# A twelve-layer decoder on one core: both ends of the state-space layer interleaved, and the norms, scores and last group of the last three layers moved

## The chip, the cores and the metric

The kernel runs on one core of a Trainium2 chip. The metric is the device time of one execution in microseconds; the median of three runs is used. The core has five instruction streams that run beside each other: TensorE (PE, matrix products and transposes, results in PSUM), VectorE (DVE), ScalarE (ACT), GpSimd (POOL) and SyncE (SP, which here only starts transfers). Each works through its own queue in order, and a semaphore makes an instruction wait for another engine or a transfer.

## The reference

A residual stream x of 32 sequences x 128 tokens x 128 channels (fp32) goes through twelve sublayers, each of them added to x after a norm without weights:

```python
def _layernorm(x, axis=-1, eps=1e-05):
    m = jnp.mean(x, axis=axis, keepdims=True)
    v = jnp.var(x, axis=axis, keepdims=True)
    return (x - m) / jnp.sqrt(v + eps)

x = x + _L0_attn_ref(_layernorm(x), ...)    # state-space layer (layer0 in the kernel)
x = x + _L0_xattn_ref(_layernorm(x), ctx, ...)  # 8-head attention over x and ctx (layer1)
...
x = x + _L3_attn_ref(_layernorm(x), ...)    # sparsemax attention on 32 patterns (layer9)
x = x + _L3_xattn_ref(_layernorm(x), ctx, ctx, dropout_mask, Wout, bout, 32)  # layer10
x = x + _L3_ffn_ref(_layernorm(x), weight_q, weight_scale, bias)              # layer11
```

The state-space layer has a projection, a causal convolution over four tokens, a gate, a decay dt per head, a scan over the tokens, a gated norm with weights and an output projection. The sparsemax attention needs 32 scores per head and token in sorted order:

```python
z_sorted = -jnp.sort(-z, axis=-1)
cum = jnp.cumsum(z_sorted, axis=-1)
tau = (cum_sel - 1.0) / k_sup          # from the largest k that is still in the support
A = jnp.maximum(z - tau, 0.0)
```

Layer10 is a softmax attention with a dropout mask: `softmax(x ctx^T / 32) * mask`, times ctx, times Wout. Layer11 quantizes each token to int8 by its largest absolute value, multiplies with int8 weights and scales back:

```python
x_scale = jnp.maximum(amax, EPS) / 127.0
x_q = jnp.clip(jnp.round(x2d / x_scale), -128, 127).astype(jnp.int8)
acc = x_q @ weight_q.T
out = acc * x_scale * weight_scale + bias
```

## The kernel before

**Tiling.** The 32 sequences are G = 8 groups of J = 4; `xg[i]` holds the residual of group i on 128 partitions (tokens) x 4 x 128, in place through the whole kernel. A "block" is one sequence of one group. Short-lived tiles come from small rings: `gmid` (10 buffers of 128x512), `bmid` (5), `bbig` (4 of 128x2048), `gbig` (3), `val`, `xn` and `xnT` (2), and in PSUM `ps`, `two` and `acc` (2 each). A tile that finds no free buffer waits until the last reader of the oldest one is done.

**Order.** The engines' queues are written out from the Python program. `Ordered` (L194 is the call in it, which is why nearly every row of the profile has that line) can tie an engine's instructions to the order of the program: `follow(T, A, V)` does so for TensorE, ACT and DVE in layer0 and in layer1. Outside of that a scheduler lays the order by its own estimates, so in the last layers the order of emission is only a hint. POOL and SP are never tied by `follow`.

**Start.** SP loads the constants `cs` (L278), then the eight groups of x (L284), three of the weight units (L304) and, since nothing holds it back, the int8 weights wq (L1691), although `layer9` writes that load. ACT's queue loads `first`, `wide`, `rows` and `small` (`ws`). DVE turns wq to bf16 once (L1692).

**layer0** runs round by round, one block per round: `first` (scores of the block and its POOL products, L805 to L812), `second`, `exponentials`, `weighted` and `third` are of consecutive blocks, and beside them the generators `conv` (four per group), `gate`, `entry` (the norm of a group), `decays` (dt) and `joined` (gated norm and output projection of a finished group) go forward by a step at a time through `go`. The loop begins at n = -9 with the steps of the first groups and ends with two rounds of `joined` for the last group. The power -1/2 of a norm is on POOL (L738, L891).

**layer1** then loads ctx (L323), normalizes (`prepare`, `normed` on POOL, L397), projects (`project_in`), makes scores, exponentials and the product with the reciprocal sum (L1020 on POOL), and enters its rounds: transposes of block n, scores of block n+1, values, `weighted`, `project_out`.

**layer9 to layer11** are one loop over i = 0 to 10 with 15 steps n each. In turn i, group i is sorted (`sort`, a merge network on DVE whose unchanged ends ACT copies), group i-1 gets its thresholds (`threshold`, TensorE, ACT, DVE and a POOL subtraction at L1753) and its `values`, group i-2 goes through layer10 and group i-3 through layer11. The norm of these three layers is `norm_act`: statistics on DVE, the power on POOL (L364), the shift on DVE, and the scaling on ACT, all emitted in one go. The scores of group i+1 are emitted at n = 10. The second half of the experts of layer8 lies in a list, `beside`, whose 49 entries are spread over the first 54 steps:

```python
slots = G // 2 * len(steps) - 6
```

In layer10 and layer11 POOL has the product with the mask (L1838), the scaling by the reciprocal sum (L1844), clipping and rounding (L1881, L1882) and the last two additions (L1896, L1897), for each group. The output of a group leaves from SP (L1898) behind its last addition.

Of the kernel before, what the change touches and what calls it, by code (L numbers as in the profile page):

```python
# [204 lines left out]
def program(ctx, tc, cols, x, ctxt, mask, drop, dfirst, dsmall, dwide, drows, dunits, dexperts, dconst, drel, dwq, out):  # L205
# [72 lines left out]
    SY.dma_start(out=cs, in_=dconst)  # L278
# [3 lines left out]
    for i in range(G):  # L282
# [3 lines left out]
        if i == 0:  # L286
            w0 = units.tile([128, cfirst.n], F32, tag="unit", name="w0")
            A.dma_start(out=w0, in_=dfirst)
            ww = const.tile([128, cwide.n], F32, name="ww")
            A.dma_start(out=ww, in_=dwide.to_broadcast([128, cwide.n]))  # L290
            wr = const.tile([1, crows.n], F32, name="wr")
            A.dma_start(out=wr, in_=drows)
# [27 lines left out]

    def load_ctx(i):
# [30 lines left out]
    def norm_act(src, o, by=None, by2=None):  # L352
# [6 lines left out]
        if by is not None:  # L359
            V.tensor_tensor(rs, mv[:, :, 1], by2, ALU.mult)  # L360
            V.tensor_scalar(rs, rs, EPS, None, ALU.add)
        else:
            V.tensor_scalar(rs, mv[:, :, 1], EPS, None, ALU.add)
        P.tensor_tensor(rs, rs, K["nhalf"], ALU.pow)  # L364
        if by is not None:
            V.tensor_tensor(rs, rs, by, ALU.mult)
        V.scalar_tensor_tensor(sh, mv[:, :, 0], -1.0, rs, ALU.mult, ALU.mult)
        for j in range(J):
            A.activation(o[:, j, :], src[:, j, :], AF.Identity, bias=sh[:, j : j + 1], scale=rs[:, j : j + 1])

    def layernorm_act(i):
        xn = mid.tile([128, J, D], F32, tag="xn", name="xn", bufs=2)
        xnT = mid.tile([128, 512], F32, tag="xnT", name="xnT", bufs=2)
        norm_act(xg[i], xn)
        transposed(xn, xnT, A.copy)
        return xnT
# [291 lines left out]
    def layer0():  # L668
# [190 lines left out]
        def joined(g):  # L859

            ys, sq = [], []
            for b in range(2):
                y = bmid((128, J, 128))
# [8 lines left out]
            for y in ys:  # L872
                q = bmid((128, J, 128))
# [10 lines left out]
            ln = bmid((128, J, 128))  # L884
            A.copy(ln, op)
            yield
# [21 lines left out]
        for n in range(-9, G * J + 2):  # L908
# [46 lines left out]
            go(conv, g, c)  # L955
        follow()

    def layer1(then):  # L960
# [12 lines left out]
        def project_in(n):  # L973
            i, j = n // J, n % J
            at = slice(j * 128, (j + 1) * 128)
            if n % 2 == 0:
                keys[n // 2] = gbig((128, 2, 4, 256))
# [81 lines left out]
        follow(T, A, V)  # L1059
        prepare(0, 0)  # L1060
        prepare(0, 1)
        project_in(0)
        for c2 in range(2):
            for step in scores(0, c2):
                step()
        prepare(1, 0)
        project_in(1)
        project_values(0)
        for n in range(last + 1):
# [10 lines left out]
            if n < last:  # L1080
# [12 lines left out]
                weighted(n)  # L1093
                if j == 0 and 0 < i and i + 1 < G:
# [3 lines left out]
        follow()  # L1098
# [590 lines left out]
    def layer9():  # L1689
        wq8 = const.tile([128, 32], I32, name="wq8")  # L1690
        SY.dma_start(out=wq8, in_=dwq)  # L1691
        V.tensor_copy(wq, wq8.bitcast(I8))  # L1692
# [16 lines left out]
        def scores(i):  # L1709
            xnT = layernorm_act(i)  # L1710
# [6 lines left out]
            ordered[i] = flat(z)  # L1717

# [36 lines left out]
        def values(i):  # L1755
            z = zs.pop(i)
# [22 lines left out]
            for j in range(J):  # L1779
                A.copy(yT[:, j], t[:, :, j])  # L1780
            project(i, yT.rearrange("p j h l -> p (j h l)"), W["a3_Wo"], WW["L3_attn_bo"])


        scores(0)
        queue = list(beside)
        slots = G // 2 * len(steps) - 6
        for i in range(G + 3):
            tails = {}
            if 0 <= i - 2 < G:
                tails |= dict(zip((1, 4, 7, 11), layer10(i - 2)))  # L1790
            if 0 <= i - 3 < G:
                tails |= dict(zip((2, 5, 8, 12), layer11(i - 3)))
            for n in range(len(steps)):
# [6 lines left out]
                if 0 <= i - 1 < G and n < 4:  # L1800
                    threshold(i - 1, n)
                if 0 <= i - 1 < G and n == 6:
                    values(i - 1)
                if i + 1 < G and n == 10:
                    scores(i + 1)
                if n in tails:
                    tails[n]()
# [9 lines left out]
    def layer10(i):  # L1817

        st = {}

# [130 lines left out]
```

## Time and profile before

| | us |
|---|---|
| runs (median of 3; lowest, highest) | 3045.65 (3045.08, 3048.45) |
| the profiled execution | 3068.78 |
| its span, first to last instruction | 3066.8 |

| engine | busy, us | share of the span |
|---|---|---|
| PE (matmul) | 2563.0 | 84% |
| PEld (weight load) | 1638.7 | 53% |
| DVE | 2086.1 | 68% |
| ACT | 1529.3 | 50% |
| POOL | 1007.4 | 33% |

The mean granted TensorE clock is 0.91. The chain of work that ended last is 49% PE, 31% DVE, 8% ACT and 6% POOL of the span. Landmarks: layer0's fill is over at about 65 us, its last block at about 443, layer1's rounds begin at 487, the first sort step stands at 2536.5, the later turns of the sort begin at 2573.4, 2641.8, 2715.1, 2778.8, 2831.9, 2888.3 and 2945.9, the last sort step ends at about 2991, and the last output is started at about 3063.

How to read it: in the slices each digit is the busy share of a fortieth of the span (77 us) in tenths; PEclk is the granted clock of TensorE in tenths. A row of the timeline begins with its start and its length, then engine, line, operation, output<-input by the program's names and shapes, and in brackets how long the engine was idle before it and what ended that. A row of waits has what waited, on what, the sum in us, how often, and the longest. A group's row has the count, the busy sum and the mean in ns of one.

### The profile page before, as it was taken

The page shows a single profiled execution, that of the slowest core. Times are in us where ns is not written, and L with a number is a line of the kernel's source. Part 1 is how long each engine was busy: PE and PEld are TensorE (multiplying, and loading weights), DVE is VectorE, ACT ScalarE, POOL GpSimd, SP SyncE. Part 2 cuts the span into 40 slices and gives each one's busy share as a digit, 9 for nine tenths or more (in the row PEclk, how much of TensorE's full clock was granted, in tenths as well). Part 3 has the DMA queues.
Part 4 walks back from the last instruction along what each step waited for, and adds up shares of the span by engine and source line. Part 5 has one row for each costly group of instructions (what it writes and reads, how often), then busy time and mean ns, then how long its engine had stood idle before and what let it go on. Part 6 is the DMA issues. An engine that isn't in the chain of part 4 may idle for free.

```text
span 3066.8 us, 55735 instructions
## 1 busy us (share of the span) xinstructions
PE 2563.0 (84%) x22535; PEld 1638.7 (53%) x22554; DVE 2086.1 (68%) x4254; ACT 1529.3 (50%) x3540; POOL 1007.4 (33%) x1042
## 2 busy tenths in 40 slices
PE   4887878999989999999998999988886869885564
PEld 2555556777744445556664444445553657543333
DVE  4776756888878856667776555468894329777883
ACT  3554544444422246666664444467771225555563
POOL 3333332322310113235441000223433445424544
PEclk7877878999999999999998999979997989998777
DMA  3000000000000000000000000000003243100000
GB/s 109 2 2 2 2 23 4 8 5 5 1 21 1 1 32 2 5 9 9 12 2 15 1 1 1 1 1 2 1 6 124 84 147 114 55 18 14 21 11 21
DMA packets 50147, 68.36 MB, mean 22 GB/s; under 512 B 3681, under 2 KB 41570, under 8 KB 49762
## 3 DMA queue, kind: packets, MB, share of 16 engines
q1 hardware_dynamic: 42608, 33.84, 3.6%
q0 software_dynamic: 6848, 27.81, 2.7%
q8 instruction: 178, 2.92, 0.4%
q10 hardware_dynamic: 434, 3.14, 0.3%
q14 instruction: 79, 0.65, 0.1%
HBM read 51.11 MB, written 13.68 MB: 21 GB/s over the span
## 4 chain that ended last, share of the span: by engine, by line
PE 49%; DVE 31%; ACT 8%; POOL 6%; issue 3%; DMA 1%; another core or an unknown queue 1%; SPq 0%; POOLq 0%; DVEq 0%; ACTq 0%
PE ps L194 22%; PE two L194 15%; PE acc L194 13%; DVE bbig L194 13%; DVE s L194 9%; DVE bmid L194 4%; DVE gmid L194 3%; ACT bbig L194 3%; POOL xn L397 3%; ACT bmid L194 2%; ACT gmid L194 1%; DVE x L194 1%; POOL s L395 1%; ACT gbig L194 1%; POOL s L364 1%
## 5 line engine op out<-in xcount | busy, mean ns | idle before, releaser
L194 PE MATMUL ps<-cs,bbig 128*128 128x128 f32 x2208 | 326.6, 287 | 82.0 <-ACT bbig L194 34.4
L194 PEld LDWEIGHTS ps<-cs,bbig 128*128 128x128 f32 x2208 | 251.8, 145 | 187.2 <-ACT bbig L194 81.0
L194 ACT COPY bbig<-ps 128x512 f32<-128x512 f32 x416 | 228.2, 590 | 247.2 <-PE ps L194 246.9
L194 DVE TENSOR_REDUCE s<-two 128x8 f32<-128x1024 f32 (+1 forms) x192 | 234.2, 1220 | 123.7 <-PE two L194 122.6
L194 DVE TENSOR_TENSOR bbig<-bbig 128x256 f32<-128x256 f32 (+4 forms) x394 | 274.0, 749 | 1.3 <-ACT bbig L194 0.3
L194 PE MATMUL two<-xnT,u 128*128 128x512 f32 x512 | 260.0, 608 | 11.8 <-ACT bmid L194 6.3
L194 PE MATMUL acc<-bmid,u 128*128 128x512 f32 x448 | 238.2, 619 | 32.8 <-DVE bmid L194 31.4
L194 PE MATMUL two<-gbig,gmid 32*128 32x512 f32 (+1 forms) x1280 | 223.1, 570 | 3.1 <-ACT bbig L194 2.4
L194 DVE TENSOR_TENSOR bmid<-bmid,ps 128x512 f32<-128x512 f32 x192 | 130.1, 684 | 108.3 <-ACT bmid L194 89.2
L194 ACT ACTIVATE bbig<-two,s 128x256 f32<-128x256 f32 (+1 forms) x512 | 189.7, 419 | 24.5 <-DVE s L194 21.2
L477 POOL TENSOR_SCALAR gbig<-bmid,cs 128x512 f32<-128x512 f32 x96 | 148.7, 1564 | 160.0 <-ACT bmid L194 160.0
L194 ACT ACTIVATE bbig<-bbig 128x512 f32<-128x512 f32 (+1 forms) x160 | 128.1, 801 | 86.6 <-DVE bbig L194 86.1
L194 ACT ACTIVATE bmid<-two 128x512 f32<-128x512 f32 x104 | 61.7, 596 | 195.4 <-PE two L194 185.4
L194 PEld LDWEIGHTS acc<-bmid,u 128*128 128x128 f32 x448 | 81.3, 195 | 134.2 <-DVE bmid L194 77.5
L194 PEld LDWEIGHTS two<-xnT,u 128*128 128x128 f32 x512 | 91.4, 191 | 114.9 <-issue 56.0
L194 ACT ACTIVATE bmid<-two,ws 128x512 f32<-128x512 f32 x128 | 85.1, 686 | 110.0 <-PE two L194 109.8
L1020 POOL TENSOR_TENSOR bbig<-bbig,s 128x1024 f32<-128x1024 f32 x32 | 60.6, 1892 | 232.5 <-PE two L194 161.0
L194 ACT ACTIVATE bbig<-bbig,s 128x128 f32<-128x128 f32 x384 | 118.7, 387 | 27.4 <-DVE s L194 27.4
L194 DVE TENSOR_TENSOR bbig<-two,s 128x1024 f32<-128x1024 f32 (+1 forms) x128 | 122.6, 958 | 8.6
L489 POOL MEMSET val<- 128x512 f32 x72 | 39.4, 550 | 262.8 <-PE acc L194 261.8
L194 ACT COPY bbig<-bbig 128x256 f32<-128x256 f32 (+3 forms) x320 | 97.8, 375 | 49.2 <-DVE bbig L194 47.2
L194 PE MATMUL ps<-cs,xn 128*128 128x128 f32 x288 | 62.0, 307 | 70.7 <-POOL xn L397 25.1
(292 smaller groups left out, 5948.3 us busy)
## 6 DMA issues: line engine op xcount, KB each, us to landing
u<-in_units SPq DMA_DIRECT2D x10, 768.0 KB
gmid<-in_ctx SPq DMA_DIRECT2D x16, 256.0 KB
xs<-bbig SPq DMA_DIRECT2D x4, 903.0 KB
xt<-xs SPq DMA_DIRECT2D x28, 129.0 KB
x<-in_x SPq DMA_DIRECT2D x8, 256.0 KB
gmid<-in_mask SPq DMA_DIRECT2D x8, 256.0 KB
ys<-bbig SPq DMA_DIRECT2D x2, 1024.0 KB
gmid<-ys SPq DMA_DIRECT2D x8, 256.0 KB
```

What stands on the lines that cost most here:

```text
L194: d = f(*args, **kwargs)
L364: P.tensor_tensor(rs, rs, K["nhalf"], ALU.pow)
L395: P.tensor_tensor(rs, rs, K["nhalf"], ALU.pow)
L397: P.tensor_scalar(xn[:, j, :], xg[i][:, j, :], mv[:, j, 0:1], rs[:, j : j + 1], ALU.subtract, ALU.mult)
L477: P.tensor_scalar(o[:, n, :], k, K["n4"][:, n : n + 1], None, ALU.mult)
L489: P.memset(o, 0.0)
L1020: (V if c2 else P).tensor_tensor(pr[:, four, :], pr[:, four, :], bc(nm[:, four], 2, 256), ALU.mult)
```

## The change

It has six parts.

1. At the start, the first group of x is loaded ahead of the constants. The load of wq is written ahead of layer0, and its conversion on DVE stands in layer1's round n = 3.
2. The rounds n = -9 to -3 of layer0 are replaced by a list of `go` calls in which the steps of the first group's four convolutions, its decays and the second group's norm alternate.
3. layer1's preparation becomes a generator, `lead`, whose first five steps stand in layer0's rounds 27 to 31 and whose last two stand between the steps of the last group's `joined`. What remains of that `joined` goes into layer1's rounds 0 to 2. The last group's tiles in `joined` come from `gmid` for `bmid`, and layer1's first keys from `bbig` for `gbig`.
4. `norm_act` is a generator with two steps (statistics and power; shift and scaling), and layers 9 to 11 emit them apart.
5. The scores of the next group are emitted in three steps at n = 4, 5 and 7, `values` in two at n = 6 and 10; `beside` gives three entries before the first scores and the rest over 49 steps.
6. In layers 10 and 11 the POOL operations named above are DVE operations for the last group (E = V).

```diff
-    SY.dma_start(out=cs, in_=dconst)
...
         if i == 0:
+            SY.dma_start(out=cs, in_=dconst)
...
-    def norm_act(src, o, by=None, by2=None):
+    def norm_act(src, o):
...
         P.tensor_tensor(rs, rs, K["nhalf"], ALU.pow)
+        yield
         V.scalar_tensor_tensor(sh, mv[:, :, 0], -1.0, rs, ALU.mult, ALU.mult)
         for j in range(J):
             A.activation(o[:, j, :], src[:, j, :], AF.Identity, bias=sh[:, j : j + 1], scale=rs[:, j : j + 1])
+        yield
...
     def layernorm_act(i):
         xn = mid.tile([128, J, D], F32, tag="xn", name="xn", bufs=2)
+        steps = norm_act(xg[i], xn)
+        next(steps)
+        yield
+        next(steps)
         xnT = mid.tile([128, 512], F32, tag="xnT", name="xnT", bufs=2)
-        norm_act(xg[i], xn)
         transposed(xn, xnT, A.copy)
-        return xnT
+        yield xnT
...
-        for n in range(-9, G * J + 2):
+
+        go(entry, 0)
+        go(entry, 0)
+        go(entry, 0)
+        go(entry, 1)
+        go(entry, 0)
+        go(decays, 0)
+        go(conv, 0, 2)
+        go(entry, 1)
+        go(decays, 0)
+        go(conv, 0, 2)
+        go(conv, 0, 3)
+        go(conv, 0, 2)
+        go(conv, 0, 3)
+        go(entry, 1)
...
+        for n in range(-2, G * J):
...
             go(conv, g, c)
+            if n >= G * J - 5:
+                next(lead)
+        go(joined, G - 1)
+        next(lead)
+        go(joined, G - 1)
+        next(lead)
+        go(joined, G - 1)
         follow()
+        return late[joined, G - 1]
...
+        def lead():
+            prepare(0, 0)
+            yield
+            prepare(0, 1)
+            yield
+            project_in(0)
+            yield
+            project_in(1)
+            yield
+            prepare(1, 0)
+            yield
+            steps = [step for c2 in range(2) for step in scores(0, c2)]
+            yield
+            steps[0]()
+            steps[2]()
+            project_values(0)
+            steps[1]()
+            steps[3]()
+            yield
...
                 weighted(n)
+                next(others, None)
+                if n == 2:
+                    for _ in others:
+                        pass
+                if n == 3:
+                    V.tensor_copy(wq, wq8.bitcast(I8))
...
-        scores(0)
         queue = list(beside)
-        slots = G // 2 * len(steps) - 6
+        for _ in range(3):
+            queue.pop(0)()
+        for _ in scores(0):
+            pass
+        slots = G // 2 * len(steps) - 11
         for i in range(G + 3):
-            tails = {}
+            todo = []
+            if 0 <= i - 1 < G:
+                todo += [(n, lambda n=n: threshold(i - 1, n)) for n in range(4)]
+                turns = values(i - 1)
+                todo += [(n, lambda: next(turns)) for n in (6, 10)]
             if 0 <= i - 2 < G:
-                tails |= dict(zip((1, 4, 7, 11), layer10(i - 2)))
+                todo += zip((1, 2, 4, 7, 11), layer10(i - 2))
             if 0 <= i - 3 < G:
-                tails |= dict(zip((2, 5, 8, 12), layer11(i - 3)))
+                todo += zip((3, 4, 6, 8, 12), layer11(i - 3))
+            if i + 1 < G:
+                first = scores(i + 1)
+                todo += [(n, lambda: next(first)) for n in (4, 5, 7)]
...
-                if i + 1 < G and n == 10:
-                    scores(i + 1)
...
     def layer10(i):
+        E = P if i < G - 1 else V
...
-            P.tensor_tensor(pr, pr, st["dm"], ALU.mult)
+            E.tensor_tensor(pr, pr, st["dm"], ALU.mult)
...
-                P.tensor_scalar(pr[:, j, :], pr[:, j, :], rec[:, j : j + 1], None, ALU.mult)
+                E.tensor_scalar(pr[:, j, :], pr[:, j, :], rec[:, j : j + 1], None, ALU.mult)
...
     def layer11(i):
+        E = P if i < G - 1 else V
...
-            P.tensor_scalar(q, q, 127.0, -128.0, ALU.min, ALU.max)
-            P.tensor_scalar(qb, q, rnd, rnd, ALU.add, ALU.subtract)
+            E.tensor_scalar(q, q, 127.0, -128.0, ALU.min, ALU.max)
+            E.tensor_scalar(qb, q, rnd, rnd, ALU.add, ALU.subtract)
...
-            P.tensor_tensor(o, o, bc(WW["qbias"], 1, J), ALU.add)
-            P.tensor_tensor(xg[i], xg[i], o, ALU.add)
+            E.tensor_tensor(o, o, bc(WW["qbias"], 1, J), ALU.add)
+            E.tensor_tensor(xg[i], xg[i], o, ALU.add)
...
     load_units(0, 1, 2, 3, 4)
-    layer0()
+    SY.dma_start(out=wq8, in_=dwq)
+    lead1, run1 = layer1()
+    rest0 = layer0(lead1)
     load_units(5)
     lead2, run2 = layer2()
-    layer1(lead2)
+    run1(rest0, lead2)
```

The order of the instructions that follows from it, engine by engine, is known before a run: between layer1's first rounds and layer9 it is the same as before on TensorE, DVE, ACT and POOL.

## The prediction

> **What bounds the kernel now.** First the page's slices: no engine is full throughout, and the bound changes by stage.
>
> ```profile
> PE   4887878999989999999998999988886869885564
> DVE  4776756888878856667776555468894329777883
> PEclk7877878999999999999998999979997989998777
> ```
>
> TensorE is at 8 or 9 almost everywhere from slice 2 to 27, but at 4 in the first slice, and it gives way to VectorE (DVE) in the last seven; slice 5 (383 to 460) dips on DVE. The change touches just these places. Next, the busy time of each engine by stretch (width, then PE, PEld, DVE, ACT, POOL, granted clock, DMA).
>
> ```profile
> 410.00:443.00 33.00, 29.23 (x764) 21.05 (x741) 19.76 (x40) 13.43 (x23) 12.52 (x15) 0.88 0.01 3
> 443.00:487.00 44.00, 27.24 (x117) 21.03 (x118) 15.56 (x51) 10.75 (x29) 18.20 (x20) 0.58 0.10 30
> 487.00:2573.00 2086.00, 1872.36 (x15159) 1185.74 (x15179) 1428.77 (x2876) 1037.83 (x2396) 614.24 (x692) 0.95 0.07 21
> 2642.00:2715.00 73.00, 63.69 (x291) 37.98 (x290) 52.04 (x91) 41.64 (x104) 24.28 (x19) 0.98 0.07 20
> 2888.00:2946.00 58.00, 34.75 (x172) 21.51 (x172) 45.55 (x97) 32.95 (x93) 26.02 (x18) 0.71 0.05 14
> ```
>
> 443 to 487 is the seam between the state-space layer and layer 1: a dependency chain, DVE busy 15.6 of 44, TensorE at clock 0.58. 2888 to 2946 is one round of the sort of the sparse attention: DVE 45.6 of 58, so about 12 idle. The middle (487 to 2573) keeps its order of instructions. Then what those DVE gaps wait for, in that round and at the fill:
>
> ```profile
> DVE bbig L194 <- ACT gbig L194: 12.5, 2, 6.3
> DVE s L194 <- POOL s L364: 6.0, 6, 1.1
> DVE x L194 <- PE ps L194: 4.5, 2, 2.3
> ```
>
> (Two rounds, 2839 to 2953.) Each round waits 6.25 us for the next group's scores, three times 1 us for the power on POOL (L364) and 2.3 for the add after the projection. From the timeline:
>
> ```profile
> 16.42 0.15 DVE L194 TENSOR_SCALAR ws<-ws 128x1 f32<-128x1 f32 x1 [4.89 <-DMA ws<-in_small]
> ...
> 25.75 0.23 DVE L194 CAST wq<-wq 128x128 bf16<-128x128 int8 x1 [2.27 <-DMA wq<-in_wq]
> ...
> 53.95 0.29 DVE L194 TENSOR_TENSOR dts<-ps,ww 128x128 f32<-128x128 f32 x1 [6.06 <-PE ps L194]
> ```
>
> DVE stands 2.27 us for a weight that is used 2,700 us later, and goes idle again and again until 54.
>
> The sum is made on the profiled execution: 3068.78 us, span 3066.8. The runs' median is 3045.65, 0.75% less, so a saving scales by 0.9925.
>
> **1. Fill of the state-space layer: -12.** Loading x0 ahead of cs buys nothing: the shift of the first norm stays behind the scaling of ws on DVE, which waits for the 1.6 MB transfer (16.42), bound by the bandwidth in either order (DMA share 0.97 from 0 to 20). So the first normed tile starts at 16.7, transposed at 19.5, as now. From there I lay the new order with the durations of the timeline: TensorE dt matmuls 1.75 (to 21.3), then convolutions 2, 3, 0 at 2.07 each (23.4, 25.4, 27.5); DVE taps, 2.3 per convolution: c2 25.2 to 27.5, c3 to 29.8, its finish 0.7 and the decay steps 1.6, c0 32.0 to 34.3, c1 from 35.2 (after its copy and scale on ACT) to 37.5, both finishes by 39.2; transposes for the first block 0.7, dt matmuls 1.9, and the add of the second group's dt at 41.9 in place of 53.95. From that add on DVE, ACT, TensorE and POOL have the same sequence in both. Of the 12.0, 2.3 is the wq cast, moved to layer 1's fourth round (0.23 on a DVE that is 78% busy there). Bounds: 7 (the cast, and half of the rest) to 14.
>
> **2. Seam to layer 1: -24.** Added to rounds 27 to 31: 8 transposes, two project_in (12 matmuls of 128 each, 3.1 us at full clock, with 2 ACT copies of 0.58 and one DVE copy of 0.69), two times 1.2 of bn_stats/aggr on DVE and 4.4 plus 1.26 on POOL. With the waits for two PSUM buffers I take 4 per project_in, 2 for the transposes, 1 for DVE: 11. TensorE idles 6 of the 20 us from 426 to 446, which takes about 4. Net +7, so the last block's DVE copy ends at 450 for 443. Next: the gated sum on DVE 3.7 (454), two reductions 1.4 each (457; the score matmuls ran meanwhile), exponentials (459), value copies 1.4, product on DVE 1.2 and on POOL 1.9 (461). The output product and the sums of squares, 4 us of TensorE, fit before 459. Layer 1's first transposes start at 461; now:
>
> ```profile
> 486.93 1.09 PE L194 MATMUL ps<-cs,bbig 128*128 128x128 f32 x8
> ```
>
> -26; the rest of the last group's norm (2.3 DVE, 1.65 ACT, and POOL) goes into three rounds bound by TensorE: +2. The ctx loads: the first is still issued near 391, the second now ahead of unit 3 in SP's queue; nothing later waits for unit 3 before layer 2. Keys in a bbig buffer: of four, one is the zeroed helper and two serve blocks, so no stall. Bounds: -12 (rounds lengthen by all 11, plus POOL's 11 us on the blocks) to -30.
>
> **3. Sort with experts beside it (2536 to 2779, four rounds): -14.** Scores sooner end waits of 6.1, 2.0 and 6.9 at the starts of rounds; two-step norms end 7.9 of POOL waits: 23. But 49 pieces of expert work now take 49 slots, not 54, and TensorE is already busy 64 of 73 in one of these rounds. Against this, three pieces stand before the first scores, and from 2500 to 2536 TensorE is busy 15 of 36. I take 60%: 14. Bounds 0 (TensorE decides) to 28 (all, and 5 of prefill).
>
> **4. Sort alone (2779 to 2991): -22.** The removable waits are 7.2, 11.4, 11.6 and 1.2 (last round, no next scores): 31.4. Residue: ACT is in order, and scores, norms and the values' hops to TensorE now stand between its sort copies; laying one round gives about 2.5 of DVE waiting for them. 31.4 - 3 x 2.5 = 24; 22 with the following.
>
> A rule speaks against this part. Rows first (DVE from 2780):
>
> ```profile
> L194 DVE TENSOR_TENSOR bbig<-bbig 128x1024 f32<-128x1024 f32 x32 | 45.8, 1454 | 0.1
> ...
> L194 DVE TENSOR_TENSOR bbig<-gbig 128x1024 f32<-128x1024 f32 x8 | 9.8, 1222 | 22.2 <-ACT gbig L194 22.2
> ```
>
> The same shape costs 1222 where POOL rests and 1454 on average. "SBUF — State Buffer", section "SBUF: two separate sides", of the Trainium skill says why: a DVE operation with two SBUF inputs and a POOL operation that reads SBUF hold one port pair in turn, each blocking the other for a whole instruction. By the rule the idle 12 us are where POOL gets its turn: my estimate of a serial round is 32 us of two-input DVE work plus 17 of POOL at their undisturbed durations, 49, so 8.5 off 57.6 and no more. By the rows alone, 45.6 + 2.5 = 48, 9.5 off. I take the rule's 8.5 for two rounds, 5 for the first: 22. Bounds 8 to 30.
>
> **5. Tail (2991 to 3067): -12.** The shift of the next norm no longer stands between the thresholds, and group 5's last scaling (qscale) goes before the last sort steps: laid out, POOL's fourth subtraction ends 10.4 after the sort, not 15.9: -5.5. After the last x add: scores' reduction no longer behind another group's norm, -2.7; POOL's queue (L1896, L1897 of group 6) no longer ahead of the last power, -1.3; x7's statistics behind group 6's add and scale, +2.3. Group 7 on DVE: product 1.27 to 0.69; add pair 2.52 to 1.38; clip and round 2.55 to 2 x 0.42 (nearest row: DVE TENSOR_SCALAR 128x512 to bf16, 416 ns; if 0.9 each, as four of 0.22, +0.9); four scalings 2.37. For the scalings "GPSIMD Engine Reference", section "Engine selection", says one-input operations run about alike on POOL: 0 gained on 2.37 + 2.55. The rows say otherwise: 340 ns for DVE's xn<-x scaling, 4 x 0.34 = 1.36 for 2.37. I go by the rows: 0.6 + 1.1 + 1.7 + 1.0 = 4.4 (by the rule 1.7). Sum 5.5 + 2.7 + 1.3 - 2.3 + 4.4 = 11.6. Bounds 5 to 17.
>
> **Sum:** 12 + 24 + 14 + 22 + 12 = 84, x 0.9925 = 83; 3045.65 - 83 = 2962.
>
> **Rivals.** A: all five parts about as worked out, 2962; for it, each gap is named in the waits and the order after closes it. Own range 2940 to 2985. B: the last layers keep their time: port collisions and ACT's queue refill the rounds (sort -10 in all, tail -5); for it, 1222 against 1454; against it, ACT is busy only 33 of 58. 12 + 24 + 10 + 5 = 51: 2995. C: the seam gains little, since blocks 27 to 31 are TensorE-bound (29 of 33) and stretch by all that is added: -12 for -24, and the fill 7: 2979. D: the norm's power gives no gain, because on POOL it now stands behind a product that waits for ACT's exponentials, with the shift on DVE ahead of the sort: the wait is moved, and the 18 of POOL waits in parts 3 and 4 stay: 2980. E, slower: ACT. Its copies feed every sort step; if a wait for TensorE between them is exposed at each of some 12 handoffs per round, at 1.65 (one xn) each, a round costs 20 of waiting for 12. With the other gains (48) it decides from 7 us per round over now in seven rounds; at 1.65 each on 12 it is 8 over now, 56 in all: 3054. Against it: DVE waits for ACT's copies 0.3 us in 212 today. F: no effect: the seam's and fill's gains are paid back by a lower clock in the middle, 3046; against it, the middle is at 0.95 with TensorE 90% busy.
>
> **Chances.** A 0.58, B 0.18, C and D 0.17, E 0.04, F 0.03. The range runs from all upper bounds half reached (2938) to B and a little (3000). A measurement tells 0.2% (6 us). Faster 0.94, same 0.02, slower 0.04.
>
> **What would show it.** Step 1: DVE's second dts add near 42. 2: layer 1's first bbig transposes near 449 (461 less 12). 3: the round starts (bbig<-gbig) without a wait, four rounds in about 228. 4: round starts 48 to 50 apart, POOL waits below 1 per round, the bbig<-bbig mean above 1454. 5: sort end to last output about 60 for 72. The prediction is wrong if rounds stay at 56 with "bbig <- ACT bbig" as the wait, or if the middle's 2086 changes.

## The result, and the profile after

The changed kernel takes 3001.57 us (median of four runs, 2999.27 to 3016.44) where the kernel before takes 3045.86: ratio 0.986, 95% interval 0.983 to 0.990. It is faster, by 44 us and not by the 83 that were forecast. A second set of runs on another chip gave 0.9875 (0.985 to 0.990).

The trace of the kernel before that the prediction read took 3068.78 us, 23 more than the median of its runs. A second trace of it (the first experiment) took 3041.36; it is the one compared with here. In the sets of runs below, the fastest and the slowest execution of the kernel before lie 0.45 to 0.8% apart, more than many of the edits are worth. So the experiments are judged by the length of stages within the traces, and by the time only where its interval tells something.

The slices of the changed kernel's page:

```profile
PE   5788889999989989999998999988876989876564
DVE  5777667888888756677786554468895339867873
PEclk8888889999999999999998999989997989997776
```

The first slice and the seam (slice 5) are fuller on DVE, and the last seven look much as before (DVE 9867873, where the prediction's page has 9777883). Two stations, from the timeline of the changed kernel: the second group's dt add, at 40.81 (predicted 41.9; 53.42 in the second trace of before), and layer 1's first transposes, at 444.03 (predicted 449; 476.00 in that trace).

```profile
40.81 0.29 DVE L194 TENSOR_TENSOR dts<-ps,ww 128x128 f32<-128x128 f32 x1 [2.20 <-PE ps L194]
444.03 3.54 PE L194 MATMUL ps<-cs,bbig 128*128 128x128 f32 x16
```

So the fill came as predicted, and the start of layer 1 came 32 us earlier than in the second trace, where 38 were forecast against the first. The last layers did not come as predicted. Busy time by stretch (width, then PE, PEld, DVE, ACT, POOL, granted clock, DMA), of the second trace of before: the three rounds of sort alone that have a next group's scores (rounds 4 to 6), the last round, and what lies behind the sort:

```profile
2754.50:2916.50 162.00, 90.71 (x500) 59.72 (x499) 135.25 (x288) 97.06 (x273) 73.16 (x53) 0.80 0.05 15
2916.50:2962.60 46.10, 24.59 (x148) 17.57 (x146) 42.90 (x76) 25.64 (x77) 21.96 (x15) 0.75 0.06 18
2962.60:3039.30 76.70, 35.93 (x212) 26.99 (x212) 23.33 (x90) 28.51 (x76) 36.55 (x35) 0.72 0.07 21
```

and the same three of the changed kernel:

```profile
2709.50:2873.70 164.20, 103.88 (x498) 66.74 (x498) 137.85 (x288) 97.07 (x274) 77.89 (x54) 0.78 0.05 15
2873.70:2927.00 53.30, 30.60 (x176) 22.96 (x176) 45.65 (x93) 27.73 (x82) 26.13 (x17) 0.80 0.06 15
2927.00:2997.50 70.50, 33.42 (x197) 25.32 (x196) 23.72 (x94) 27.62 (x74) 27.69 (x26) 0.69 0.08 23
```

The three rounds did not get shorter (162.0, 164.2), the last one grew by 7, and the stretch behind the sort gave 6 back. What DVE waits for in the three rounds (total, times, longest), from behind the first row of round 4 to the first row of round 7, so that the waits at the starts of rounds 5, 6 and 7 are in it; before (2755.8 to 2916.6):

```profile
DVE bbig L194 <- ACT gbig L194: 9.2, 3, 3.5
DVE s L194 <- POOL s L364: 9.0, 9, 1.1
DVE x L194 <- PE ps L194: 6.2, 3, 2.5
DVE s L194 <- PE acc L194: 2.3, 3, 1.2
```

and after (2710.8 to 2873.8):

```profile
DVE bbig L194 <- ACT gbig L194: 12.9, 3, 5.2
DVE bbig L194 <- ACT bbig L194: 7.4, 6, 2.4
DVE s L194 <- PE acc L194: 5.1, 5, 1.4
DVE s L194 <- POOL s L364: 0.3, 1, 0.3
```

The power's waits and the projection's waits are gone, as predicted. The wait for the next scores (bbig <- ACT gbig) has grown from 9.2 to 12.9, though they are emitted sooner; there is a new one, in which the sort waits for its own copies on ACT (bbig <- ACT bbig); and the thresholds' wait (PE acc) has grown by 2.8. In all, DVE waits 25.7 us and not 26.7, and it is busy 2.6 us more. With the same number of matmuls TensorE is busy 103.9 us for 90.7: more of them run at half clock (see "The clock").

### The profile page after: what moved, and what is told of

Its sections match the earlier page's. It is cut to its first block, busy times and chain, and to the rows that moved or that the text cites. A ratio compares the mean times of both kernels' runs of the same rounds, so it can differ in the third digit from the quotient of the medians.

```text
span 2997.5 us, 55783 instructions
## 1 busy us (share of the span) xinstructions
PE 2554.4 (85%) x22535; PEld 1638.7 (55%) x22554; DVE 2093.0 (70%) x4263; ACT 1527.0 (51%) x3540; POOL 1003.2 (33%) x1033
## 5 line engine op out<-in xcount | busy, mean ns | idle before, releaser
L194 PE MATMUL two<-gbig,gmid 32*128 32x512 f32 (+1 forms) x1248 | 217.1, 570 | 2.4 <-ACT bbig L194 2.4
L194 PE MATMUL ps<-cs,xn 128*128 128x128 f32 x288 | 68.9, 321 | 105.8 <-ACT xn L194 80.5
L194 PE MATMUL two<-xT,we 128*128 128x256 f32 x448 | 109.8, 400 | 8.6 <-ACT xT L194 4.2
```

What stands on the lines that cost most here:

```text
L194: d = f(*args, **kwargs)
```

## The experiments

In the expectations, "the three rounds" are rounds 4 to 6 as above. All kernels below compute everything that the kernel before computes.

**The parts, each alone.** The kernel before once more, then with one part of the change at a time: the fill; the seam (layer 1's lead in the last blocks, the rest of the last gated sum in its first rounds); the last three layers.

> The kernel before, once more, for its trace. The profiled execution that the prediction was made on took 3068.78 us, 23 more than the median of its runs, while the changed kernel's profiled execution (2999.27) lies at its runs' median. Theory 1, that one execution was slow in the state-space layer by its clock (0.80 to 0.82 there, 0.85 to 0.88 in the changed kernel for the same instructions): this trace takes 3044 to 3050, layer 1 starts near 470 and not 486.93, and its clock up to there is about 0.85. Theory 2, the change itself raises the clock in the state-space layer: layer 1 starts near 487 again, and the missing 23 us are spread elsewhere.

> The kernel before with the state-space layer's new order of entry, cs behind x0 and the 8-bit weight loaded early, and nothing else. By the prediction: 12 less, 3034. By the two traces: the second add to dts 13.1 earlier, 3032 if it is kept to the end. If later waits take it up: 3046.

> The kernel before with layer 1's first steps put among the last blocks of the state-space layer, and the rest of the last gated sum in layer 1's first rounds, and nothing else. By the prediction: 24 less, 3022. By the two traces (offset of after against before: -27 at 326 us, -20 at 419, -42 at 548, so about 7 us of added work in rounds 27 to 31 and 22 back at the start of layer 1): 15 less, 3031. Rival C of the prediction: 12 less, 3034.

> The kernel before with the changed norms, order of steps and slots of the last three layers and the last group's parts on DVE, and nothing else. By the prediction: 14 + 22 + 12 = 48 less, 2998. By rival B: 15 less, 3031. By the two traces from 2366 us on: 18 less, 3028, with 11 in the four mixed rounds, 3 in the three rounds of sort alone, 8 lost in the last sort round and 5 gained behind it.

Measured: the second trace takes 3041.36, with layer 1 at 476.00 and not 486.93; 11 of the 27 us between the two traces of the same program lie in the state-space layer (clock 0.81 and 0.83 from 150 us to the end of the seam), most of the rest just ahead of the sort. Theory 1 holds in kind, but the start of layer 1 lies between the two numbers, and the clock is not all of it.

Fill alone: ratio 0.9949 (0.993 to 0.997), 16 less. Seam alone: 0.9936 (0.992 to 0.996), 20 less. Last layers alone: 0.999 (0.998 to 1.000), 3 less, where the prediction has 48. The product of the three is 0.9875, so the parts add up, and all of the miss lies in the last layers. The first two rest on the medians: the profiled execution of the fill alone (3039.92) was the slowest of its four runs, and in its trace the 13.7 us gained at 117 us are lost again by 370 us, in blocks at clock 0.79 from 150 to 400 us (0.86 in the second trace of before). The trace of the seam alone shows 10 us less at 598 us.

In the last-layers trace the four rounds with expert work (the mixed rounds) take 228.5 for 241.7, the three rounds 167.4 for 162.1, the last 54.1 for 46.1, the end 70.6 for 76.7; and its first sort step comes 5.7 later against the work ahead of it, where the three expert pieces now stand before the first scores.

**When the scores are emitted.** Edits to the changed kernel, in the table of steps and in `scores`:

```diff
-                todo += [(n, lambda: next(first)) for n in (4, 5, 7)]
+ late:          todo += [(n, lambda: next(first)) for n in (9, 10, 10)]
+ norm early:    ... for n in ((0, 1, 7) if i > 3 else (4, 5, 7))]
+ free:          ... for n in (4, 5, 5, 6)]
+ both:          ... for n in ((0, 1, 5, 6) if i > 3 else (4, 5, 5, 6))]
  (free and both, in scores:)
-            qT = linearT(W["a3_Wq"], xnT, W["L3_attn_bq"])
+            qT, p = gmid(), two()
+            mm(p[:, 0, :], W["a3_Wq"], xnT)
+            A.activation(qT, p[:, 0, :], AF.Identity, bias=W["L3_attn_bq"])
+            yield
...
-                p = ps()
-                mm(p, qT[:, j * 128 : (j + 1) * 128], flat(kb))
+                (two products into each of two tiles two(), one A.mul each)
```

> The changed kernel with the three steps of the next group's scores moved from steps 4, 5 and 7 of a round to 9, 10 and 10, about where the kernel before emits them; all else as changed. Theory P (the scores' earlier place gives nothing, since TensorE does them behind the values and the cross attention's transposes anyway): the three rounds of sort alone stay at 162 to 168, the time at 2996 to 3006. Theory of the prediction (the earlier place is what takes the wait away, and something else refilled it): the wait at the start of each round grows from 4.5 to 8 or more, the three rounds to 176, the time by 15 to 25.

> The changed kernel with the norm of the next group's scores at steps 0 and 1 of a round in place of 4 and 5, in the rounds without expert work only (4 to 6). In the changed kernel TensorE stands 6.7 us on average (39.9 in 6 waits) for a normed tile in these rounds, with the values' transposes behind it. Theory P (TensorE's order puts values and scores behind a tile that is late by POOL's product): that wait falls below 2 a piece, the round starts no longer wait for the scores (4.5 each now), the three rounds go from 164 to about 150, the time from 3001 to 2987. Theory Q (VectorE and POOL hold each other, a round can't go below about 54): the waits move but the three rounds stay at 161 to 166.

> The changed kernel with the scores' query projection and products in the PSUM tiles that the experts use (two), not in the two tiles (ps) that all else shares, emitted at steps 5 and 6; the norm stays at 4 and 5. Theory P2 (the scores are late because their PSUM tiles come in turn behind those of the values and of the cross attention): TensorE does them between the values' hops, the start of each round no longer waits for them, and each of the three rounds is 4 to 5 shorter: about 151, time 2988. Theory Q as for the early norm: 161 to 166. In the four mixed rounds the experts use the same tiles, so these may grow by 0 to 5.

> Both of the last two edits together. Theories P and P2: the scores are in place before the values, neither holds up the other, the starts of rounds 5, 6 and 7 wait for nothing, and a round is what VectorE is busy (46) plus 2.5: the three 145, the time 2983. Theory Q: the three rounds stay at 161 to 166 and VectorE's rows get longer (bbig<-bbig 128x1024 above 1.45 us).

| | three rounds, us | clock there | wait for scores at the starts of rounds 5 to 7 | for sort copies (bbig <- ACT bbig) | for POOL and projection | ratio |
|---|---|---|---|---|---|---|
| changed | 164.2 | 0.78 | 12.9 | 7.4 | 0.3 | 0.986 |
| scores late | 153.1 | 0.80 | 0 | 1.8 | 13.2 | 0.9855 |
| norm early | 167.4 | 0.74 | 0 | 18.4 | 3.3 | 0.9884 |
| scores free | 171.4 | 0.76 | 0 | 19.5 | 6.8 | 0.9866 |
| both | 165.4 | 0.80 | 0 | 22.6 | 3.6 | 0.9868 |

Scores emitted late made the rounds the shortest of these, and their wait is gone; both theories said no. (The whole time tells nothing here: this kernel's four mixed rounds took 236.4 for 231.5.) The reason stands in TensorE's waits of the changed kernel:

```profile
PE ps L194 <- ACT xn L194: 39.9, 6, 8.9
PE acc L194 <- ACT bmid L194: 4.5, 9, 0.8
```

and in its timeline, round 6 (it began at 2818.97):

```profile
2847.30 0.86 PE L194 MATMUL ps<-cs,xn 128*128 128x128 f32 x2 [8.93 <-ACT xn L194]
...
2849.05 0.58 ACT L194 COPY xnT<-ps 128x512 f32<-128x512 f32 x1
...
2864.75 1.92 PE L194 MATMUL ps<-xnT,ws 128*128 128x512 f32 x2
...
2867.44 5.60 PE L194 MATMUL ps<-kb,gmid 128*128 128x512 f32 x8 [0.78 <-ACT gmid L194]
...
2873.71 1.23 DVE L194 TENSOR_TENSOR bbig<-gbig 128x1024 f32<-128x1024 f32 x1 [5.21 <-ACT gbig L194]
```

TensorE stands 8.93 us for the next group's normed tile (xn), with the values of the group before behind it, whose last input was ready at 2839.5. Then the scores' transposed tile (xnT) is copied at 2849.05 and used at 2864.75: the values' steps and the cross attention's transposes come first, in the same two PSUM tiles. Emitted late, nothing of the scores stands ahead of the values, they begin 18 to 19 us into the round and not 29 to 31, and the scores are done about when the sort is. That falsifies the prediction's step: the early place did not take the wait away (8.8 to 16.0 us in the four traces with this order, 0 with the late place); put where it was, it held up the chain that the scores hang on.

The other three took the wait at the round starts away too, as theories P and P2 said, and the rounds did not get shorter: the waits for sort copies grew by 11 to 15 us. From the timeline of the kernel with both edits:

```profile
2858.20 0.77 ACT L194 COPY gmid<-ps 128x128 f32<-128x128 f32 x4 [0.35 <-PE ps L194]
2859.31 0.34 ACT L194 COPY bbig<-bbig 128x64 f32<-128x64 f32 x1
2859.69 2.82 DVE L194 TENSOR_TENSOR bbig<-bbig 128x1024 f32<-128x1024 f32 x3 [8.37 <-ACT bbig L194]
```

DVE stands 8.37 us for a sort copy of 0.34. On ACT it comes behind 18 other operations, from 2850.45 on; eleven of them are the values' copies, in a chain that goes to TensorE and back five times. This is the mechanism of rival E of the prediction: a queue in order, with a chain of hand-offs ahead of what DVE needs. Of theory Q (DVE and POOL hold each other) one sign is there: the 128x1024 rows of the sort take 1536 ns on average over the last four rounds with both edits, 1522 with the early norm, 1354 in the changed kernel. But DVE's busy time in the three rounds is 137.5 with both edits and 137.9 in the changed kernel, so it is the waits, not the rows, that hold the rounds at 55.

**Which cure.** The norm's statistics, the normed tile and the scores are set apart ("apart"); the values are emitted in four pieces ("pieces"); both; and, for the end, the last group's parts go back to POOL:

```diff
+ apart:   todo += [(n, lambda: next(first)) for n in (4, 8, 10)]
+ pieces:  in values, a yield ahead of the copies to rows, one at c == 2
+          among them, and one ahead of the last transposes;
-          todo += [(n, lambda: next(turns)) for n in (6, 10)]
+          todo += [(n, lambda: next(turns)) for n in (6, 7, 8, 9, 11)]
+ POOL:    E = P   (in layer10 and layer11, for all groups)
```

> The changed kernel with the next group's statistics at step 4 of a round, its normed tile at 8 and its scores at 10 (changed: 4, 5, 7; with 9, 10, 10 the three rounds of sort alone took 153.1 in place of 164.2, with one wait of 3.2 a round for POOL's power left). Theory R (what counts in a round is that TensorE and ACT begin the values early, with no normed tile in front of them; the power may come early): the POOL wait goes too, the three rounds take 145 to 150, the time 2990. Theory E (ACT in order: each wait that is removed lays a sort copy bare behind the values' steps on ACT): the waits for ACT's sort copies grow to 10 or more and the three rounds stay at 153 or longer.

> The changed kernel with the values given out in four pieces, at steps 6, 7, 8 and 9, and their projection at 11 (changed: all at 6, projection at 10); the scores stay at 4, 5 and 7. Theory E (VectorE's waits of 2 to 5 for a sort copy come from ACT's queue, where the values' copies, each waiting for TensorE, stand ahead of it): the waits for ACT's sort copies fall from 7.4 in the three rounds to 3 or less, and the round start's wait stays; the three rounds take 158 to 161. Theory R (the values begin late, behind the normed tile): the waits move, the three rounds stay at 162 to 166.

> Both of the last two edits together. Theories R and E agree here: values early and in pieces, no wait for scores, power or sort copies, the three rounds at VectorE's 46 a round plus 2, 144 to 146, the time 2984. If VectorE and POOL hold each other (the rule of the prediction: 49 a round): 147 to 150, with longer rows on VectorE.

> The changed kernel with the last group's product, scalings, clip, rounding and last two sums back on POOL. By the prediction's rows the stretch behind the sort grows by 4.4; by the rule that one-input operations run about alike on POOL, by 1.7; by the two traces (product 0.69 for 1.27, scalings 0.88 for 2.37, clip and rounding 0.86 for 2.55, last sums 1.38 for 2.52) by 4.9. The stretch takes 70.5 now, so 75 to 75.5; the time of all runs cannot tell it (0.15%).

Measured, three rounds (clock; waits for ACT's sort copies): apart 169.9 (0.72; 22.5), pieces 152.4 (0.82; 4.5), both 175.8 (0.73; 27.4). Ratios 0.9895, 0.9832, 0.9931. Theory R falls: with the normed tile out of the way and the power early, the sort copies are bare again. The pieces work, but not only as theory E had it: the waits for sort copies fell from 7.4 to 4.5, and the wait at the round starts, which E left in place, from 12.9 to 1.8. With the values' last copies emitted after the scores, the scheduler puts them there on TensorE and ACT: a round's end in the second trace of this kernel (the next sort step begins at 2810.99):

```profile
2809.50 0.60 ACT L194 ACTIVATE gbig<-ps 128x512 f32<-128x512 f32 x1 [0.35 <-PE ps L194]
...
2810.36 0.60 ACT L194 ACTIVATE gbig<-ps 128x512 f32<-128x512 f32 x1 [0.27 <-PE ps L194]
2810.85 0.56 ACT L194 COPY gbig<-ps 32x512 f32<-32x512 f32 x1
2810.99 2.36 DVE L194 TENSOR_TENSOR bbig<-gbig 128x1024 f32<-128x1024 f32 x2 [0.61 <-ACT gbig L194]
```

My reading is that the two waits come from one chain and that the pieces cut it in the middle: the scores pass, and ACT has no more than half of the hand-offs in a row. TensorE still stands 8.9 us for the normed tile. The reading is not complete: both theories had the two edits together at 144 to 146, and they gave the longest rounds of all, with 27.4 us of waits for sort copies although the values came in pieces. Why they did so is open. What goes with the length is TensorE's busy time for the same matmuls (498 or 499): pieces 96.5 us, changed 103.9, apart 111.4, both 113.1.

The last group on POOL: the stretch behind the sort takes 75.0 us, for 70.5 and 70.6 in the two traces of the changed kernel, so DVE is worth 4.5. (The ratio, 0.9888 with 0.985 to 0.993, cannot tell it.) From the timelines, clip and rounding on POOL:

```profile
3002.80 0.62 POOL L1974 TENSOR_SCALAR bmid<-bmid 128x512 f32<-128x512 f32 x1 [4.47 <-ACT bmid L194]
3003.51 1.93 POOL L1975 TENSOR_SCALAR gmid<-bmid 128x512 bf16<-128x512 f32 x1
```

and on DVE, in the changed kernel:

```profile
2988.50 0.43 DVE L194 TENSOR_SCALAR bmid<-bmid 128x512 f32<-128x512 f32 x1 [1.40 <-ACT bmid L194]
2988.97 0.43 DVE L194 TENSOR_SCALAR gmid<-bmid 128x512 bf16<-128x512 f32 x1
```

But the three rounds, in which this kernel has the changed kernel's order on TensorE, ACT, DVE and POOL alike (as the last-layers one has on TensorE, ACT and DVE), took 157.8 in this trace for 164.2 and 167.4: the next question.

**The clock.** Same order, three rounds, clock, TensorE's busy time: 157.8, 0.82, 98.5; 164.2, 0.78, 103.9; 167.4, 0.76, 108.2. Rounds and busy time differ by the same 10 us. Counted from the clock records of the traces, TensorE works at half clock for 27 us of the three rounds before, 50 in the changed kernel, 35 with the pieces and 73 with pieces and apart together. In windows of 2 us, from the changed kernel's round 5 (width, then PE, PEld, DVE, ACT, POOL, granted clock, DMA):

```profile
2773.70:2775.70 2.00, 0.84 (x8) 0.64 (x6) 2.00 (x7) 0.62 (x2) 1.30 (x2) 1.00 0.94 272
2775.70:2777.70 2.00, 0.00 (x0) 0.00 (x0) 2.00 (x6) 0.00 (x0) 1.50 (x1) 1.00 0.05 13
2777.70:2779.70 2.00, 0.00 (x0) 0.00 (x0) 1.66 (x3) 0.06 (x1) 1.89 (x2) 0.86 0.00 0
2779.70:2781.70 2.00, 1.51 (x7) 1.51 (x8) 2.00 (x2) 1.59 (x4) 0.33 (x1) 0.50 0.00 0
2781.70:2783.70 2.00, 1.65 (x8) 1.25 (x7) 1.59 (x10) 1.93 (x5) 1.30 (x1) 0.50 0.04 8
2783.70:2785.70 2.00, 2.00 (x12) 2.00 (x11) 1.07 (x4) 1.86 (x6) 0.30 (x1) 0.50 0.00 0
2785.70:2787.70 2.00, 0.50 (x3) 0.30 (x2) 2.00 (x4) 0.00 (x0) 2.00 (x2) 0.93 0.00 0
```

The clock is 1.00 or 0.50 (0.86 and 0.93 are windows in which it changes). TensorE's last matmul ends at 2774.5, and by the 0.86 the clock halves at 2779.1, 4.6 us later; work begins at 2780.2, and by the 0.93 the clock is whole at 2786.0, after 5.8 us. "TensorE: Matmul & The Clock Gate", section "What's actually happening", of the Trainium skill says so: half rate after one idle window of about 3.4 us, full rate after a busy one, in a window that runs free of the program. The rows agree with it, as they come out at more than one such window each way; that the free window is what makes one execution differ from the next is likely and not shown. To raise the clock, matmuls that nothing needs:

```diff
                 if i < G:
+                    if i >= 4:
+                        for _ in range(1):      # two in the second kernel
+                            mm(two()[:, 0], ident, ordered[i][:, 0:512])
                     sort(i, n)
```

> The changed kernel with one more matmul of 128x512 at each sort step of rounds 4 to 7 (identity times what the step reads, into a PSUM tile that nobody reads): work added that nothing needs, to keep TensorE from standing idle. In windows of 2 us the trace of the changed kernel shows TensorE's clock at 1.00 or 0.50 and little between: 0.50 from about 4 us after it went idle until some 4 us after it is dense again. Theory G (in these rounds the values, scores and cross attention run at half clock behind such gaps, and that is what makes the scores late and ACT's queue long): the clock of the three rounds rises from 0.78 to 0.90 or more, they take 140 to 155 in place of 158 to 167, the time falls by 10 to 20, though 15 matmuls a round are added. Rival H (the clock follows and does not set; ACT's order sets the round): the three rounds stay at 158 to 170 or grow.

> As the last, with two added matmuls at each step. Theory G: clock 0.95 or more; the three rounds 140 to 155, unless the added 18 us of TensorE a round stand ahead of the chain. Rival H: longer than with one.

> The kernel before with the one added matmul at each sort step of rounds 4 to 7. Theory G: its three rounds (162 at clock 0.80, 167 at 0.755) fall to 150 to 158 too, less than in the changed kernel, since its POOL waits (9.0) and projection waits (6.2) stay. Rival H: 162 to 168.

> The changed kernel with the values in four pieces (three rounds 152.4, clock 0.82) and the one added matmul at each sort step of rounds 4 to 7. Theory G and E together: no wait left on ACT or on scores, the three rounds near VectorE's 46 a round, 140 to 148, the time 2980 to 2990 on a chip where the kernel before takes 3045. Rival H: 150 to 156.

Measured, three rounds (clock): 163.6 (0.91), 172.3 (0.97), before 168.6 (0.88), pieces 156.8 (0.89). Ratios 0.9868, 0.9874, 0.9999, 0.9838. The clock rises as theory G said, and the rounds stay or grow, as rival H said. It is no clean test of the clock: with one a step TensorE waits 15.7 us in the three rounds with an added matmul at its head, for DVE, and it is busy 24.5 us more. What it shows is that matmuls added in this way do not mend the rounds; whether a higher clock alone would is open.

**The better kernel.** The changed kernel and the one with the values in pieces, again, on one chip:

> The changed kernel once more, beside the next one on the same chip, for a second trace and more runs: ratio to the kernel before 0.986 as at first. If the three rounds of sort alone follow TensorE's clock in that stretch (same order: 157.8 at 0.82, 164.2 at 0.78, 167.4 at 0.76): 161 at 0.80, and 1.6 less for each 0.01 of clock more.

> The changed kernel with the values in four pieces, once more, against the changed kernel on the same chip. Theory E (ACT's queue, mended by the pieces): the three rounds 150 to 156, the stretch from the first sort step to the end 504 to 510 (changed kernel 518 to 521), the ratio to the kernel before 0.982 for 0.986. If the first trace of it was only one with a high clock (0.82): the three rounds 156 to 164 and the ratio 0.985 to 0.988.

Measured: changed 3005.79 us, 0.9875 (0.985 to 0.990), three rounds 164.1 at clock 0.77; pieces 2993.17, 0.9833 (0.981 to 0.985), three rounds 153.2 at 0.82, from the first sort step to the end 502.6 for 517.2. DVE's waits in the three rounds, with the pieces (2711.3 to 2863.2):

```profile
DVE bbig L194 <- ACT bbig L194: 4.5, 3, 1.9
DVE x L194 <- PE ps L194: 3.4, 6, 1.1
DVE s L194 <- PE acc L194: 2.5, 5, 0.5
DVE bbig L194 <- ACT gbig L194: 1.8, 3, 0.6
```

So it is no accident of one trace: the kernel with the pieces is 13 us faster than the changed one and 53 faster than the one before. Its clock was 0.82 both times. By the slope of the changed order (157.8 at 0.82, 164.1 at 0.77) some 6 of the 11 us go with the clock and 5 do not; whether the clock is higher because the chain is shorter, or by chance, two traces do not settle. The late scores gave three rounds as short as these (153.1), in a single trace; the pieces together with the late scores are not among the runs.

## Why the prediction was wrong, point by point

- **Step 1, fill, -12: right.** -12.6 at the dt add, -13.6 from there through the blocks, 16 by the medians of the fill alone (its own trace lost them again, at a lower clock).
- **Step 2, seam, -24: right in kind, too large.** -17 between the two traces (the changed kernel is 13.6 ahead in the blocks and 30.8 at 598 us), 20 by the medians of the seam alone. The added work cost 9 and not 7 (last block's third copy 427.54 against 431.97, with 13.6 of fill gained); from there to layer 1's transposes it takes 16.5 for 44.0, where the prediction had 11.
- **Step 3, mixed rounds, -14: half.** The four rounds take 10 to 13 less (231.5 and 228.4 for 241.7), but 3.3 to 5.7 of it goes to the three pieces ahead of the first scores, which the step named and did not price apart.
- **Step 4, sort alone, -22: failed, and it decides.** "Residue: [...] laying one round gives about 2.5 of DVE waiting for them" was wrong. Of the waits it called removable, 20.6 us are left in the three rounds (12.9 for scores, 7.4 for sort copies, 0.3 for the power) and not 7.5; the thresholds' wait grew by 2.8 and DVE's work by 2.6, and with the last round the stretch grew by some 9 in place of shrinking by 22. Those for POOL's power and the projection went (15.2 before, 0.3 after). That for the scores did not: emitted early, their normed tile holds up TensorE ahead of the values, and the scores come behind both; emitted late, as the kernel with late scores shows, they left no such wait. The step looked at the last wait of the scores and not at what TensorE and ACT have ahead of them. The rounds stayed at 54 to 55, near the 56 that the prediction named as its sign of being wrong, with "bbig <- ACT bbig" as one of two waits and not the only one. Besides, there was less to remove: the 30.2 us that the step found in the three rounds of the first trace (7.2 + 11.4 + 11.6) are 24.4 in the second (9.2 + 9.0 + 6.2).
- **Step 5, tail, -12: half, and lost again.** Behind the sort -6.2. The parts on DVE are worth 4.5: the rows were right (4.4), and the rule on one-input operations (1.7) was not. Sort to values' sum gave 3.5 for 5.5; from there to the cross attention's sum nothing, since x7's statistics and power, behind group 6's sums on DVE and POOL, come 3.2 later after its last sum. The last sort round, which the step took as unchanged, took 53.3 for 46.1 (54.1 in three other traces of this order): DVE's work in it is 2.8 us more, and it waits for ACT's sort copies:

```profile
2910.08 2.26 DVE L194 TENSOR_TENSOR bbig<-bbig 128x448 f32<-128x448 f32 x4 [4.74 <-ACT bbig L194]
```

- **The rivals.** B came nearest (2995), in part by luck: its -10 for the sort was about 0 in the traces (449.8 to 449.0 from the first sort step to the last). Its refill by ACT's queue is what the trace shows; its port collisions are not: the 128x1024 rows have a mean of 1354 ns from the first round of sort alone on, for 1455 in the second trace of before, so the "mean above 1454" was wrong. Nor does POOL rest where the prediction read 1222 ns: at the starts of rounds 5 to 7 of the first trace a POOL operation (L636, two inputs) begins 0.4 us into that row and takes 1.93 us, for 1.27 where it is alone; there it is POOL that is longer. The estimate of 49 a round as a floor remains untested, since the shortest round of all took 49.9. E's mechanism was right too, its size was not: in the changed kernel the sort waits for ACT's copies six times in three rounds, up to 2.4 us, and not twelve times a round; in the kernels with the early norm or the free scores single waits of 5.8 to 8.4 cost what these edits gained. D's prediction for DVE fell (0.3 us of POOL waits left), but the late power that it described is part of what holds TensorE for 8.93 us. In round 6 the statistics end at 2841.9 on DVE, POOL takes the power behind a product that waited for ACT, and DVE has the shift only at 2846.33:

```profile
2842.67 1.40 POOL L1928 TENSOR_TENSOR bmid<-bmid,gmid 128x512 f32<-128x512 f32 x1 [2.00 <-ACT bmid L194]
...
2844.18 1.31 POOL L364 TENSOR_TENSOR s<-s,cs 128x4 f32<-128x4 f32 x1
```

- **The base.** Two traces of the same program differ by 27 us; a sum of 84 had to be read against that. Of the 42 us between the two traces compared here, 7 lie between 598 and 2310 us, where the order is the same; 5 of these are one delay near 2305 us in the second trace of before, which the traces of the single parts do not have.
- **The range.** Its lower end (2938) does not follow from the bounds shown: they add up to 119, and halfway from 84 to that is 101, which gives 2945. The miss lies at the other end.

## What to carry to other kernels

Before a wait is priced as removable, follow the late value back through every queue that it crosses, and ask what stands ahead of it there and what will be ahead of others when it is moved; here the same chain, cut in the middle, gave what moving its end forward did not. An edit that takes one wait away and leaves the round as long has uncovered a second wait of equal rank; here two such edits put together did not shorten the rounds either, so the pair has to be measured as well. And look at a mean clock of 0.7 to 0.8 in windows of 2 us: here it is a switch between 1.00 and 0.50, and a gap of 4.6 us put the work behind it at half clock.

## What the runs showed that was not expected

- The same order of instructions on every engine took 157.8 to 167.4 us in one stretch, with TensorE's clock at 0.82 to 0.76.
- Rounding to bfloat16 in 128x512 takes 1.93 us on POOL and 0.43 on DVE, the clip ahead of it 0.62 and 0.43: of these two one-input operations only the one with a change of type is far slower on POOL. The four scalings of 128x128 take 2.37 and 0.88.
- Matmuls added to an engine that is idle 37% of the time raised its clock from 0.78 to 0.97 and lengthened the rounds from 164 to 172.
